# A perceiver layer on one core: the opening's loads put into one queue, and the context's channels dealt to chunks by fours

## The chip, the cores and the metric

The kernel runs on one core of a Trainium2 chip, as one launch. The metric is the device time of that core in microseconds (us). Times of the runs are given as a median. The profile is one profiled execution of the program.

## What is computed

The layer takes 256 tokens `x` of 512 channels and a context of 25088 tokens of 512 channels, all float32. It has three parts, each added to its input. The first part, cross attention, takes most of the time and is the one the change touches:

```python
def xattn(q, k, v, Wq, bq, Wk, bk, Wv, bv):      # k = v = context
    qp = q @ Wq.T + bq                            # 256 x 128
    kp = k @ Wk.T + bk                            # 25088 x 128
    vp = v @ Wv.T + bv                            # 25088 x 512
    z = sigmoid(qp @ kp.T / sqrt(128))            # 256 x 25088
    return z @ vp

x = x + xattn(layernorm(x), context, context, ...)
x = x + causal_attention(layernorm(x), ...)       # 16 heads of 64, one key and value head
x = x + mixture_of_experts(layernorm(x), ...)     # 64 experts, 8 per token, and a shared one
```

There is no softmax in the cross attention, so `z @ (v @ Wv.T)` is built as `(z @ v) @ Wv.T`: the loop over the context only sums `z @ context`, and the value weights are applied once, behind the loop.

## The kernel before, in words

**Tiles and groups.** The context is cut into 66 groups: group 0 has one block of 128 tokens, the 65 others have three blocks (J = 3) of 128 tokens. Each group needs its context twice. As `ctx_g`, tokens lie on the 128 partitions; this feeds the sum `z @ context`. As `cT_g`, channels lie on the partitions; this feeds the keys, because TensorE sums over partitions. `cT_g` has four chunks of 128 channels (ND = 4), and the keys of a group are four matmuls, one for each chunk, that are summed in PSUM: `keys(g)`, line 389.

**Two ways to `cT`.** Groups 0 and 1 are transposed by TensorE (`turn_by_pe`, line 355), which turns whole 128 x 128 blocks of `ctx_g` against the identity matrix `ident`; the result goes to PSUM, and ScalarE and VectorE copy it to `cT` (lines 377 and 379). A chunk there is 128 neighbouring channels. From group 2 on (BY_PE = 2), VectorE transposes (`turn`, line 351). For that the context is read a second time from memory, as `quarters_g` (`load_quarters`, line 123): four transfers, each of which puts a quarter of the channels (128 of them) on 32 partitions. One transpose instruction at line 353 turns all 32 x 32 squares of it: 1536 elements on each partition. There, chunk c holds channels 32c to 32c+31 of each of the four quarters.

**Two copies of the key weights.** The channels of a chunk thus differ between the two ways, and so must the rows of the key weights. `wk_plain` (line 149) has the rows in plain order and serves groups 0 and 1; `wkT_sb` (lines 154 to 159, four transfers) has them as VectorE's chunks need them, and serves the rest. `keys` picks one at line 385.

**The loop.** For each g, lines 666 to 694: VectorE's sums of context blocks (`context_sums`, the tile T) and, by GpSimd and ScalarE, the rest of them for the next group; scores `pz` (line 409) and their sigmoid on ScalarE into `zT` (line 418); the keys of the next group; the products `xacc` (line 610) of the group before, as a fast 3 x 3 scheme with fewer products that needs the sums S and T; VectorE's sums S of `zT`; the transpose for group g+2; and the loads for group g+3 at the top. `in_turn` keeps the order of the program on an engine for the instructions it wraps; what is not wrapped is placed by a scheduler.

**The opening.** `x` arrives in two halves of 128 tokens, one on the queue of SyncE (SP) and one on ScalarE's (lines 145 and 146). Then SP loads `ctx_0`, `wk_plain`, `ctx_1` (one transfer), `quarters_2`, `wkT_sb`, `ctx_2`; ScalarE's queue loads `wqT`; GpSimd's the two biases. Meanwhile TensorE multiplies zeros (`keep_warm`, line 621). VectorE finds mean and variance of both halves of `x` and normalizes them into `xn` (lines 623 to 630). TensorE turns `ctx_0` (line 631), then `xn` (line 638), whose transpose `xnT` is copied by both engines (line 643); then come the keys of group 0, the queries `pq` (line 651, four matmuls of 256 tokens) with their bias (line 660), and the transposes of `ctx_1` (line 661). The loop follows.

Of the kernel before, what the change touches and what calls it, by code (L numbers as in the profile page):

```python
# [22 lines left out]
def tile_perceiver_layer(  # L23
# [71 lines left out]

    idle_sb = cpool.tile([P, J, D], F32, tag="ctx", name="idle_sb", bufs=5)[:, 0, :]
    in_turn(nc.vector.memset(idle_sb, 0.0))

# [14 lines left out]
    def blocks_of(g):  # L115

        return range(J) if g > 0 else (1,)

    def tokens_of(g):
        lo = HEAD + (g - 1) * J * P if g > 0 else 0  # L120
        return context[lo : lo + len(blocks_of(g)) * P, :]

    def load_quarters(g):

        q = cpool.tile([P, J * P // R, D // NA], F32, tag="quarters", name=f"quarters_{g}", bufs=3)
        for a in range(NA):
            nc.sync.dma_start(
                q[a * R : (a + 1) * R, :, :],
                tokens_of(g).rearrange("(b i) (a d) -> a i b d", i=R, a=NA)[a],
            )  # L130
        quarter_tiles[g] = q

    def load_context(g):
        t = cpool.tile([P, J, D], F32, tag="ctx", name=f"ctx_{g}", bufs=5)
        blocks = blocks_of(g)
        nc.sync.dma_start(
            t[:, blocks[0] : blocks[-1] + 1, :],
            tokens_of(g).rearrange("(j p) d -> p j d", p=P),
        )
        ctx_tiles[g] = t  # L140


    BY_PE = 2
    x_sb = act.tile([P, NT, D], F32, tag="x", name="x_sb")
    for t, queue in enumerate((nc.sync, nc.scalar)):
        queue.dma_start(x_sb[:, t, :], x[t * P : (t + 1) * P, :])
    load_context(0)
    wqT_sb = load("wqT", [P, ND, QK], rows(wqT), queue=nc.scalar)
    wk_plain_sb = load("wk_plain", [P, ND, QK], rows(wkT), cpool)
    bk_sb = load("bk", [QK, 1], bk, queue=nc.gpsimd)  # L150
    bq_sb = load("bq", [QK, 1], bq, queue=nc.gpsimd)
    load_context(1)
    load_quarters(2)
    wkT_sb = const.tile([P, ND, QK], F32, tag="wkT", name="wkT_sb")
    for a in range(NA):
        nc.sync.dma_start(
            wkT_sb[a * R : (a + 1) * R, :, :],
            wkT.rearrange("(a c r) e -> a r c e", a=NA, r=R)[a],
        )
    load_context(2)  # L160


    def later(name, shape, *parts, halves=False):
# [68 lines left out]

    ident = const.tile([P, P], F32, tag="ident", name="ident")
    make_identity(nc, ident)
    eps_sb = const.tile([P, 1], F32, tag="eps", name="eps_sb")
    nc.vector.memset(eps_sb, EPS)
    ones_sb = const.tile([P, 1], BF16, tag="ones", name="ones_sb")
    nc.vector.memset(ones_sb, 1.0)

# [15 lines left out]
    token_n = const.tile([P, NT], mybir.dt.int32, tag="token_n", name="token_n")  # L255
    nc.gpsimd.iota(token_n, pattern=[[P, NT]], base=0, channel_multiplier=1)
    tokens_sb = const.tile([P, NT], BF16, tag="tokens", name="tokens_sb")
    const.tile([P, 16], F32, tag="spacer", name="spacer")
    nc.gpsimd.tensor_copy(tokens_sb, token_n)

    tri = const.tile([P, 2, P], F32, tag="tri", name="tri")
# [88 lines left out]

    def turn(g):
        q = quarter_tiles.pop(g)
        in_turn(nc.vector.transpose(new_turned(g), q.rearrange("p b (c r) -> p c b r", r=R)))  # L353

    def turn_by_pe(g):

        cT = new_turned(g)
        blocks = blocks_of(g)
        n = len(blocks)

        many = 512 // (n * P)
        for lo in range(0, ND, many):
            pt = sum_bank(f"ptc_{g}_{lo}")[:, 0 : many * n * P]
            for c in range(lo, lo + many):
                for i, k in enumerate(blocks):
                    at = ((c - lo) * n + i) * P
                    in_turn(
                        nc.tensor.transpose(
                            pt[:, at : at + P],
                            ctx_tiles[g][:, k, c * P : (c + 1) * P],  # L370
                            ident,
                        )
                    )
            to = cT[:, lo : lo + many, 0 : n * P // R, :]
            src = pt.rearrange("p (c b r) -> p c b r", c=many, r=R)
            if lo % 2:
                in_turn(nc.vector.tensor_copy(to, src))
            else:
                in_turn(nc.scalar.copy(to, src))

    def keys(g):

        cT = turned_tiles.pop(g)
        n = len(blocks_of(g)) * P
        w = wkT_sb if g >= BY_PE else wk_plain_sb
        pk = keys_bank(f"pk_{g}")[:, 0:n]
        for c in range(ND):
            in_turn(
                nc.tensor.matmul(  # L389
                    pk,  # L390
                    lhsT=w[:, c, :],
                    rhs=cT[:, c, 0 : n // R, :].rearrange("p b r -> p (b r)"),
                    start=(c == 0),
                    stop=(c == ND - 1),
                )
            )
        kT = cpool.tile([QK, J * P], F32, tag="kT", name=f"kT_{g}")

        for lo, hi in ((0, P), (P, n)) if 0 < g < 3 else ((0, n),):
            in_turn(nc.scalar.activation(kT[:, lo:hi], pk[:, lo:hi], AF.Identity, bias=bk_sb))  # L400
        return kT
# [217 lines left out]
            opened.add(i)  # L619

    keep_warm(D, D, 3 * P)
    xn = work.tile([P, NT, D], F32, tag="tok", name="xn")
    found = [moments(x_sb[:, t, :], f"x{t}") for t in range(NT)]
    for t, (mean, sd, rs) in enumerate(found):
        in_turn(nc.vector.reciprocal(rs, sd))
        in_turn(
            nc.vector.tensor_scalar(
                xn[:, t, :], x_sb[:, t, :], mean, rs, ALU.subtract, ALU.mult
            )
        )  # L630
    turn_by_pe(0)
    xnT = work.tile([P, ND, T], F32, tag="tokT", name="xnT")
    pxs = [sum_bank(f"pt_xn_{c}") for c in range(0, ND, 2)]
    for t in range(NT):
        for c in range(ND):
            at = (c % 2) * T + t * P
            in_turn(
                nc.tensor.transpose(
                    pxs[c // 2][:, at : at + P], xn[:, t, c * P : (c + 1) * P], ident
                )  # L640
            )
    for i, copy in enumerate((nc.vector.tensor_copy, nc.scalar.copy)):
        in_turn(copy(xnT[:, 2 * i : 2 * i + 2, :].rearrange("p c t -> p (c t)"), pxs[i]))

    warm = small.tile([P, 1], F32, tag="warm", name="warm_0", bufs=1)
    in_turn(nc.scalar.activation(warm, eps_sb, AF.Sigmoid))
    kT = keys(0)
    pq = sum_bank("pq")
    for c in range(ND):
        in_turn(  # L650
            nc.tensor.matmul(
                pq[:, :T],
                lhsT=wqT_sb[:, c, :],
                rhs=xnT[:, c, :],
                start=(c == 0),
                stop=(c == ND - 1),
            )
        )
    qT = cpool.tile([QK, T], F32, tag="qT", name="qT", bufs=1)
    in_turn(nc.vector.tensor_scalar(qT, pq[:, :T], bq_sb, None, ALU.add))  # L660
    turn_by_pe(1)
    open_products()


# [1611 lines left out]
```

## Time and profile before

| what | before |
|---|---|
| median of 3 runs | 750.83 us (750.47 to 751.04) |
| the profiled execution's own time | 751.11 us |
| its span (first to last instruction) | 749.2 us |
| TensorE matmul busy (PE) | 742.1 us (99%) |
| TensorE weight load busy (PEld) | 615.9 us (82%) |
| VectorE busy (DVE) | 598.2 us (80%) |
| ScalarE busy (ACT) | 209.5 us (28%) |
| GpSimd busy (POOL) | 210.1 us (28%) |
| moved by DMA | 148.66 MB, mean 198 GB/s |
| granted TensorE clock, mean | 1.000 |

How to read it: a row of groups names line, engine, operation, output and inputs, shapes and how often, then busy us and mean ns of one, then the engine's idle time just before them and what ended it. A row of the timeline is start, duration, engine, line, operation and how many were merged, with the idle time before it in brackets. A row of the windows has PE, PEld, DVE, ACT and POOL busy us (and instructions), the granted clock, the DMA engines' share and GB/s. PE overlaps PEld. The ends of matmuls are modelled, so that a busy PE need not be at its peak, and the matmuls of a row may overlap.

### The profile page before, as it was taken

How to read it: one execution, taken by the hardware profiler on the slowest of the kernel's cores; microseconds unless marked ns; L12 is line 12 of the kernel's file. 1: busy time of each engine (PE TensorE's matmuls, PEld its weight loads, DVE VectorE, ACT ScalarE, POOL GpSimd, SP SyncE). 2: the span in 40 equal slices, each digit the busy share in tenths (PEclk: the TensorE clock that was granted, in tenths of full speed). 3: DMA queues.
4: the chain of work that ended last, by engine and by line, in shares of the span. 5: the costliest groups of instructions: out<-in, count | busy, mean ns of one | idle time of the engine just before them, and what ended most of it. 6: DMA issues, size and time to landing. Idle time of an engine off the chain costs nothing.

```text
span 749.2 us, 12967 instructions
## 1 busy us (share of the span) xinstructions
PE 742.1 (99%) x4238; PEld 615.9 (82%) x4238; DVE 598.2 (80%) x1733; ACT 209.5 (28%) x509; POOL 210.1 (28%) x406
## 2 busy tenths in 40 slices
PE   8999999999999999999999999999999999999997
PEld 6888888888888888888888888888878679987775
DVE  5987888788788878888887888788776678986576
ACT  4222222222222222222222222222236632112110
POOL 3222232223223222322222222223212610561451
PEclk9999999999999999999999999999999999999999
DMA  9998877887799999999987887885034005998762
GB/s 247 269 238 212 199 185 180 210 199 172 197 257 210 219 207 250 256 224 211 227 196 199 202 189 171 212 199 136 1 108 146 2 29 193 389 384 278 271 180 82
DMA packets 156165, 148.66 MB, mean 198 GB/s; under 512 B 8326, under 2 KB 113939, under 8 KB 156096
## 3 DMA queue, kind: packets, MB, share of 16 engines
q1 hardware_dynamic: 153184, 140.28, 74.5%
q0 software_dynamic: 2240, 7.02, 2.9%
q8 instruction: 34, 0.56, 0.3%
q10 hardware_dynamic: 672, 0.52, 0.2%
q14 instruction: 35, 0.29, 0.2%
HBM read 145.63 MB, written 2.16 MB: 197 GB/s over the span
## 4 chain that ended last, share of the span: by engine, by line
PE 97%; DMA 1%; DVE 1%; SPq 0%; ACT 0%; issue 0%
PE xacc L610 38%; PE pk L389 22%; PE pz L409 11%; PE ph_e L1489 5%; PE seven L1611 4%; PE pa L1014 2%; PE ph_few L2039 2%; PE pw L1086 2%; PE ph_s L1489 2%; DMA ctx<-in_context 1%; PE po_few L2069 1%; PE ph_first L1408 1%; PE pd_last L1680 1%; PE ph_second L1408 1%; PE ph_e L1408 1%; PE ps L1112 1%
## 5 line engine op out<-in xcount | busy, mean ns | idle before, releaser
L610 PE MATMUL xacc<-T,S 128*128 128x172 f32 (+2 forms) x912 | 185.5, 308 | 0.0
L389 PE MATMUL pk<-cT,wkT_sb 128*128 128x384 f32 x512 | 175.5, 486 | 0.0
L610 PEld LDWEIGHTS xacc<-T,S 128*128 128x128 f32 x912 | 152.5, 190 | 20.1
L389 PEld LDWEIGHTS pk<-cT,wkT_sb 128*128 128x128 f32 x512 | 97.1, 190 | 54.4
L577 POOL TENSOR_TENSOR T<-ctx 128x172 f32<-128x172 f32 x65 | 31.9, 491 | 382.3 <-PE xacc L610 376.0
L577 DVE TENSOR_TENSOR T<-ctx 128x172 f32<-128x172 f32 (+1 forms) x262 | 113.8, 435 | 0.0
L353 DVE STREAM_TRANSPOSE cT<-quarters 128x1536 f32<-128x1536 f32 x64 | 113.3, 1771 | 0.3 <-issue 0.3
L577 DVE TENSOR_TENSOR S<-zT 128x128 f32<-128x128 f32 x196 | 56.4, 288 | 71.0 <-ACT zT L418 71.0
L409 PE MATMUL pz<-qT,kT 128*128 128x256 f32 x392 | 106.1, 379 | 0.0
L418 ACT ACTIVATE zT<-pz 128x256 f32<-128x256 f32 (+1 forms) x131 | 64.2, 490 | 113.6 <-PE pz L409 113.6
L610 PE MATMUL xacc<-T,zT 128*128 128x173 f32 (+1 forms) x396 | 89.9, 308 | 0.0
L400 ACT ACTIVATE kT<-pk,bk 128x384 f32<-128x384 f32 (+2 forms) x68 | 38.4, 568 | 146.9 <-PE pk L389 146.9
L610 PE MATMUL xacc<-ctx,S 128*128 128x172 f32 x392 | 78.5, 309 | 0.0
L587 ACT COPY T<-ctx 128x170 f32<-128x170 f32 (+1 forms) x130 | 43.4, 336 | 124.8 <-PE xacc L610 123.4
L577 DVE TENSOR_TENSOR S<-zT,S 128x128 f32<-128x128 f32 x325 | 76.3, 284 | 0.0
L577 POOL TENSOR_TENSOR T<-ctx,T 128x170 f32<-128x170 f32 (+1 forms) x130 | 72.4, 575 | 0.0
L577 DVE TENSOR_TENSOR T<-ctx,T 128x172 f32<-128x172 f32 x195 | 65.4, 361 | 8.2 <-PE xacc L610 1.5
L409 PEld LDWEIGHTS pz<-qT,kT 128*128 128x128 f32 x392 | 68.5, 190 | 3.8 <-ACT kT L400 0.2
L610 PEld LDWEIGHTS xacc<-T,zT 128*128 128x128 f32 x396 | 66.4, 190 | 0.3
L610 PEld LDWEIGHTS xacc<-ctx,S 128*128 128x128 f32 x392 | 62.8, 190 | 0.1
L610 PE MATMUL xacc<-ctx,zT 128*128 128x170 f32 (+1 forms) x264 | 59.5, 307 | 0.0
L610 PEld LDWEIGHTS xacc<-ctx,zT 128*128 128x128 f32 x264 | 44.3, 189 | 0.3
(355 smaller groups left out, 846.6 us busy)
## 6 DMA issues: line engine op xcount, KB each, us to landing
ctx<-in_context SPq DMA_DIRECT2D x65, 768.0 KB, 5.3
quarters<-in_context SPq DMA_DIRECT2D x256, 192.0 KB, 6.8
gu<-in_e_gate_up SPq DMA_DIRECT2D x12, 1024.0 KB, 9.3
gu_s<-in_s_gate_up SPq DMA_DIRECT2D x8, 512.0 KB, 11.4
dn<-in_e_down SPq DMA_DIRECT2D x7, 512.0 KB
a_wqT<-in_a_wqT SPq DMA_DIRECT2D x4, 512.0 KB
a_wout<-in_a_woutT SPq DMA_DIRECT2D x2, 1024.0 KB
dn_s<-in_s_down SPq DMA_DIRECT2D x4, 512.0 KB
```

Source lines behind the costliest of these rows:

```text
L353: in_turn(nc.vector.transpose(new_turned(g), q.rearrange("p b (c r) -> p c b r", r=R)))
L389: nc.tensor.matmul(pk, lhsT=w[:, c, :], rhs=cT[:, c, 0 : n // R, :].rearrange("p b r -> p (b r)"), start=(c == 0), stop=(c == ND - 1),)
L400: in_turn(nc.scalar.activation(kT[:, lo:hi], pk[:, lo:hi], AF.Identity, bias=bk_sb))
L409: nc.tensor.matmul(pz[:, i * T : (i + 1) * T], lhsT=kT[:, at : at + P], rhs=qT, start=True, stop=True,)
L418: nc.scalar.activation(zT[:, blocks[0] : blocks[-1] + 1, :].rearrange("p j t -> p (j t)"), pz[:, 0 : len(blocks) * T], AF.Sigmoid, scale=1 ...
L577: in_turn(f(o_, a_, b_))
L587: in_turn(nc.scalar.copy(named[to][:, 0:n], named[x_][:, 0:n]))
L610: nc.tensor.matmul(banks_of_products[i][:, cols], lhsT=named[lhs], rhs=named[rhs][:, 0:n],  start=i not in opened, stop=(g == G - 1 and last),
L1014: nc.tensor.matmul(pa[:, 0 : hi - lo], lhsT=a_wqT_sb[:, c, e * P : (e + 1) * P], rhs=anT[:, c, lo:hi], start=(c == 0), stop=(c == ND - 1),)
L1408: nc.tensor.matmul(ph[:, f * T + lo : f * T + hi], lhsT=gu[:, c, col : col + P], rhs=fT[:, c, lo:hi], start=(c == 0), stop=(c == ND - 1),)
L1489: nc.tensor.matmul(to[:, f * P : (f + 1) * P], lhsT=lhs[:, c, f * P : (f + 1) * P], rhs=rhs[:, c, :], start=(c == 0), stop=(c == HALVES - 1),)
L1611: nc.tensor.matmul(product_of_seven(nm), lhsT=block(n, hT, dn, s_, t_, lhs), rhs=block(n, hT, dn, s_, t_, rhs),  start=(n == SEVEN[0] and ...
```

## The change

Three things are changed.

The loads of the opening go into one queue, SP's, and keep the order of the program: both halves of `x`, `ctx_0`, the key weights, the query weights, the three blocks of `ctx_1` as three transfers, `quarters_2`, `ctx_2`. The loads up to group 5 keep their order too. The query and key weights are read with four neighbouring rows to a partition.

A chunk of channels is now every fourth channel: chunk c holds channels c, c+4, c+8 and so on. TensorE's transposes of the opening read `ctx` and `xn` with a step of four floats; VectorE's transpose reads each quarter with a step of four floats in place of runs of 32. Its output is as before. Since all groups have the same chunks, one copy of the key weights is left.

The opening's work is cut anew: `xn`, `xnT` and the queries go by halves of 128 tokens; `ctx_1` is turned block by block, with copies shared out by block; a dummy square root is run on ScalarE at the start, and the dummy sigmoid comes after the keys' copy of group 0. A spacer in the constants is halved.

```diff
-    for t, queue in enumerate((nc.sync, nc.scalar)):
-        queue.dma_start(x_sb[:, t, :], x[t * P : (t + 1) * P, :])
+    for t in range(NT):
+        in_turn(nc.sync.dma_start(x_sb[:, t, :], x[t * P : (t + 1) * P, :]))
     load_context(0)
-    wqT_sb = load("wqT", [P, ND, QK], rows(wqT), queue=nc.scalar)
-    wk_plain_sb = load("wk_plain", [P, ND, QK], rows(wkT), cpool)
+    wkT_sb = const.tile([P, ND, QK], F32, tag="wkT", name="wkT_sb")
+    in_turn(nc.sync.dma_start(wkT_sb, wkT.rearrange("(p c) e -> p c e", c=ND)))
+    wqT_sb = const.tile([P, ND, QK], F32, tag="wqT", name="wqT_sb")
+    in_turn(nc.sync.dma_start(wqT_sb, wqT.rearrange("(p c) e -> p c e", c=ND)))
+    ctx_tiles[1] = cpool.tile([P, J, D], F32, tag="ctx", name="ctx_1", bufs=5)
+    for k in blocks_of(1):
+        in_turn(nc.sync.dma_start(ctx_tiles[1][:, k, :], tokens_of(1)[k * P : (k + 1) * P, :]))
+    load_quarters(2)
+    load_context(2)
     bk_sb = load("bk", [QK, 1], bk, queue=nc.gpsimd)
     bq_sb = load("bq", [QK, 1], bq, queue=nc.gpsimd)
-    load_context(1)
-    load_quarters(2)
-    wkT_sb = const.tile([P, ND, QK], F32, tag="wkT", name="wkT_sb")
-    for a in range(NA):
-        nc.sync.dma_start(
-            wkT_sb[a * R : (a + 1) * R, :, :],
-            wkT.rearrange("(a c r) e -> a r c e", a=NA, r=R)[a],
-        )
-    load_context(2)
+    warm_sd = small.tile([P, 1], F32, tag="warm_sd", name="warm_sd", bufs=1)
+    in_turn(nc.scalar.activation(warm_sd, eps_sb, AF.Sqrt))
...
-    const.tile([P, 16], F32, tag="spacer", name="spacer")
+    const.tile([P, 8], F32, tag="spacer", name="spacer")
...
     def turn(g):
         q = quarter_tiles.pop(g)
-        in_turn(nc.vector.transpose(new_turned(g), q.rearrange("p b (c r) -> p c b r", r=R)))
+        in_turn(nc.vector.transpose(new_turned(g), q.rearrange("p b (r c) -> p c b r", r=R)))
...
+    def turn_by_pe(g, copies):
...
+        for i, k in enumerate(blocks):
+            pt = sum_bank(f"ptc_{g}_{k}")
+            parts = ctx_tiles[g][:, k, :].rearrange("p (d c) -> p c d", c=ND)
+            for c in range(ND):
+                in_turn(nc.tensor.transpose(pt[:, c * P : (c + 1) * P], parts[:, c], ident))
+            src = pt.rearrange("p (c b r) -> p c b r", c=ND, r=R)
+            for lo, hi, copy in copies[i]:
+                to = cT[:, lo:hi, i * P // R : (i + 1) * P // R, :]
+                in_turn(copy(to, src[:, lo:hi]))
...
-        w = wkT_sb if g >= BY_PE else wk_plain_sb
...
-                    lhsT=w[:, c, :],
+                    lhsT=wkT_sb[:, c, :],
...
+    def turn_xn(t):
+        pt = sum_bank(f"pt_xn_{t}")
+        parts = xn[:, t, :].rearrange("p (d c) -> p c d", c=ND)
+        for c in range(ND):
+            in_turn(nc.tensor.transpose(pt[:, c * P : (c + 1) * P], parts[:, c], ident))
+        pc = pt.rearrange("p (c q) -> p c q", c=ND)
+        for lo, hi, copy in (
+            ((0, ND, by_act),) if t == 0 else ((0, ND // 2, by_vector), (ND // 2, ND, by_act))
+        ):
+            in_turn(copy(xnT[:, lo:hi, t * P : (t + 1) * P], pc[:, lo:hi]))
...
+    turn_by_pe(0, [((0, ND, by_act),)])
...
+    turn_xn(0)
+    turn_xn(1)
+    kT = keys(0)
     warm = small.tile([P, 1], F32, tag="warm", name="warm_0", bufs=1)
     in_turn(nc.scalar.activation(warm, eps_sb, AF.Sigmoid))
...
+    for t in range(NT):
+        tokens_ = slice(t * P, (t + 1) * P)
+        pq = sum_bank(f"pq_{t}")[:, 0:P]
+        for c in range(ND):
+            in_turn(
+                nc.tensor.matmul(
+                    pq,
+                    lhsT=wqT_sb[:, c, :],
+                    rhs=xnT[:, c, tokens_],
+                    start=(c == 0),
+                    stop=(c == ND - 1),
+                )
+            )
+        in_turn(nc.vector.tensor_scalar(qT[:, tokens_], pq, bq_sb, None, ALU.add))
+    half = ND // 2
+    turn_by_pe(
+        1,
+        [
+            ((0, ND, by_act),),
+            ((0, ND, by_vector),),
+            ((0, half, by_act), (half, ND, by_vector)),
+        ],
+    )
```

## The prediction, made before the result was known

> **What bounds the kernel now.** I read the profile in this order: page and chain for the bound, one group of the loop for the slack of each engine, the opening's timeline for what the change touches, and the DMA rate there. The page's shares of the chain, and the longest DMA piece of the chain in order of time:
>
> ```profile
> PE 97%; DMA 1%; DVE 1%; SPq 0%; ACT 0%; issue 0%
> ...
> 2.15 9.09 DMA ctx<-in_context
> ```
>
> TensorE carries the end; the one DMA piece is group 1's context, landing at 11.24 us. One group of the loop (PE, PEld, DVE, ACT, POOL busy, clock, DMA share, GB/s), then the DVE rows that matter in it:
>
> ```profile
> 100.00:108.23 8.23, 8.23 (x46) 7.01 (x45) 6.85 (x21) 2.23 (x5) 2.06 (x4) 1.00 0.81 188
> ...
> L353 DVE STREAM_TRANSPOSE cT<-quarters 128x1536 f32<-128x1536 f32 x64 | 113.3, 1771 | 0.3 <-issue 0.3
> ...
> L577 DVE TENSOR_TENSOR S<-zT 128x128 f32<-128x128 f32 x196 | 56.4, 288 | 71.0 <-ACT zT L418 71.0
> ```
>
> PE has no gap in the 8.23 us of a group, at full clock. So only two things can move the time: when this dense stream begins, and whether another engine's group grows past 8.23. VectorE is the nearest, at 6.85: it transposes once a group (1.77) and then idles for zT, 71.0 us over some 64 groups, about 1.1 each. The opening, PE and then DVE:
>
> ```profile
> 5.80 0.60 PE L368 MATMUL ptc<-ident,ctx 128*128 128x128 f32 x4
> 7.21 1.31 PE L638 MATMUL pt_xn<-ident,xn 128*128 128x128 f32 x8 [0.82 <-DVE xn L627]
> 8.36 1.06 PE L389 MATMUL pk<-cT,wk_plain 128*128 128x128 f32 x8
> 9.25 1.89 PE L651 MATMUL pq<-xnT,wqT 128*128 128x256 f32 x8
> 11.28 1.53 PE L368 MATMUL ptc<-ident,ctx 128*128 128x128 f32 x12
> 12.65 0.60 PE L409 MATMUL pz<-qT,kT 128*128 128x256 f32 x2
> 13.08 1.13 PE L389 MATMUL pk<-cT,wk_plain 128*128 128x384 f32 x3
> ...
> 4.82 0.69 DVE L281 BATCH_NORM_STATS2 st_x<-x_sb 128x6 f32<-128x512 f32 x1 [2.99 <-DMA x_sb<-in_x]
> ...
> 6.61 0.55 DVE L627 TENSOR_SCALAR xn<-x_sb,mv_x,rs_x 128x512 f32<-128x512 f32 x1
> ```
>
> PE loses 0.8 us waiting for xn, which waits for x (4.82), and about 0.25 us at 11.28 waiting for ctx_1. From 13.08 on it is dense. Whatever the opening gains is therefore the advance of that 13.08. Rates (last figure GB/s), two queues at 2 to 4 us, one queue at 8 and 15:
>
> ```profile
> 2.00:3.00 1.00, 1.00 (x2) 0.34 (x1) 0.00 (x0) 0.97 (x1) 0.99 (x5) 1.00 0.76 266
> 3.00:4.00 1.00, 1.00 (x2) 0.34 (x1) 0.00 (x0) 0.00 (x0) 1.00 (x7) 1.00 0.86 289
> 8.00:9.00 1.00, 1.00 (x10) 1.00 (x11) 0.66 (x1) 0.44 (x1) 0.00 (x0) 1.00 1.05 377
> 15.00:16.00 1.00, 1.00 (x6) 0.72 (x5) 1.00 (x1) 0.14 (x1) 0.00 (x0) 1.00 1.03 396
> ```
>
> One queue alone is not slower than two.
>
> **The change, part by part.** *One queue in order of need.* Up to ctx_1 both kernels move 2.1 MB (x 2, context 1, weights 2, ctx_1 3 pieces of 256 KB). Before, the halves of x share the engines: 0.52 MB at about 280 GB/s from 2.05 us is 1.9, data until 3.95, BN at 4.82, so 0.87 from data to use. In line, x0's 0.26 MB takes 0.95 us: data at 3.0, use at 3.9 (estimate). SP issues every 0.46 us, faster than a piece at 280 to 377 GB/s (0.94 to 0.70): the eighth goes out at 4.0 and holds nothing up. Eight pieces end at 7.6 to 9.5, landed by 8.5 to 10.4. ACT's two issues (0.41 and 0.45) disappear ahead of a table load at 1.69 that nobody waited for: nothing gained. In the built program's order each quarter transfer of group 2 now waits on SP for the transfer eight before it (x0 first, at 3.9); behind it in SP's queue stand only later loads, and over a megabyte is still queued for the DMA engines then: no cost. Group 2's quarters then land near 13, used by VectorE at about 13.5 and by PE at pk of group 2, 17.7; a slip under 2.4 us is covered.
>
> *PE's opening again.* The warm-up still ends at 5.80. Four context transposes at 0.114 each ((12.65-11.28)/12): 6.26. The first xn transpose came 2.39 after BN (7.21-4.82): 3.9+2.39 = 6.3, so PE has its data as it comes free. The second half came 0.65 later, pk 0.50 after that: 7.44. pk to pq 0.89 (9.25-8.36): 8.33. pq in two halves of four 128-column matmuls costs pk's 0.89 each, as eight of 0.222 did before (1.78): 10.11. Twelve transposes, 1.37: 11.48, ctx_1 having landed. pz starts there, 0.43 earlier than pk could: 11.91, but pk(1) now needs all three blocks copied: last transpose 11.48, ACT copy 0.2 later, 256 columns at 0.39 (from 384 at 0.48 and 512 at 0.57), so pk at 12.15. Against 13.08: **0.93 us earlier**. DVE's copies (0.69 and 0.4) end at about 12.5; pk's third pair needs the last at 13.4: hidden. The copy that waits for ACT (halves of one tile) is counted in that. The Sqrt warming and table order are hidden: kT is needed at 11.5, made before the 1.28 load near 9. If ACT loaded first, kT would come at about 10.5, still in time.
>
> *One key copy.* Four transfers of 64 KB (SP 7.15 to 11.56) vanish, 0.26 MB; pk(2) at 18.64 did not wait for them: no time, but ctx_2 gets room.
>
> *Turn with every fourth channel.* Same 1536 elements, same single instruction, 64 times; only the source's inner step goes from 1 to 4 floats, 16 bytes. No row in this trace reads so. Nearest row: the same transpose at 1.771, of which about 0.15 is fixed (T 172 elements 0.336, S 128 elements 0.288), so 1.05 ns an element. [...] I take the nearest row, 1.77: it is the same instruction, element count and destination, and its old source already jumped every 32 elements without a price that shows. [...]
>
> *24 strided PE transposes in the opening.* The data is the weight load, 0.140 in the trace with unit step; 16-byte step: between +0 and +0.14 each, at most 3.4 us, all on PE's path. I take 0, since loads of 190 ns elsewhere lie beside their matmuls; nothing in the trace settles it. Address shifts (32 or 2048 bytes), the moved eps and the spacer: 0; the loop's order on all engines is unchanged in the built program, tail included.
>
> Sum: profiled execution 751.11 (span 749.2 and 1.9 around it) - 0.93 = 750.18; the median of the runs is 0.28 lower, 750.83, so **749.9**.
>
> **The rivals.** *VectorE becomes the bound (slower).* Mechanism: the strided read makes the transpose at line 353 longer. Up to the idle 1.1 (so a transpose of about 2.9 us, 1.64 times now) zT's wait shrinks and nothing happens; +50% (2.58) is still hidden. [...] Chance 0.22.
>
> *The opening gains nothing:* x lands no earlier when alone, or the late copies of ctx_1 eat it. With BN at 4.82, pk(1) comes at 12.15+0.92 = 13.07: 750.8. Speaks for it: the first packets come at a fixed time, and 0.87 us of the wait is not data. 0.12 (750.3 to 751.2).
>
> *Strided weight loads show:* 24 times 0.07 to 0.14 is 1.7 to 3.4, so 751.6 to 753.3. 0.08, half of it within 0.2% of before.
>
> *More than the sum:* gaps of 0.2 at groups 1 and 2 close too: under 749.3. 0.05.
>
> **How the numbers follow.** Likeliest: 749.9, own range 749.3 to 750.6, chance 0.53, of which 0.07 is under 749.33. 0.2% is 1.5 us, about what a measurement can tell from no change. Faster: 0.07+0.05 = 0.12. Within: 0.46+0.12+0.04 = 0.62. Slower: 0.22+0.04 = 0.26. The range: 749.2 leaves 0.05 below; spread evenly over 765 to 781, the VectorE case has 0.15 above 770. So 749.2 to 770.
>
> **What would show it.** Right: BN of x0 near 3.9, no PE idle before xn, ctx_1's transposes at about 10.1, pk(1) at about 12.15, a group still 8.23 us, the transpose row still 1771 ns. Wrong: that row over 2900 ns with DVE's wait for zT gone and a group of 8.5 or more (VectorE); weight loads over 140 ns in the opening (strided loads); BN still near 4.8 (no gain).

## The result and the profile after

The changed kernel takes 754.46 us (median of 6 runs, 754.18 to 755.53), the kernel before 750.61 beside it (6 runs, 750.06 to 751.04). The ratio is 1.005, with a 95% interval of 1.004 to 1.006: slower by 3.85 us, where 0.9 less was forecast. The profiled execution took 754.42, its span 752.6. A second profile and set of runs of the same kernel (e12 below) gave 754.38.

The chain of the page, then one group of the loop, then the two VectorE rows that answer to those of before:

```profile
PE 94%; DVE 3%; DMA 2%; SPq 1%; issue 0%; ACT 0%; DVEq 0%
```

```profile
100.00:108.23 8.23, 8.23 (x45) 6.94 (x44) 7.99 (x21) 2.23 (x5) 2.19 (x4) 1.00 0.73 191
```

```profile
L361 DVE STREAM_TRANSPOSE cT<-quarters 128x1536 f32<-128x1536 f32 x64 | 191.5, 2993 | 0.8 <-DMA quarters<-in_context 0.8
...
L572 DVE TENSOR_TENSOR S<-zT 128x128 f32<-128x128 f32 x196 | 65.8, 336 | 21.2 <-ACT zT L413 21.1
```

Three things are to be seen. The transpose takes 2993 ns in place of 1771. VectorE's busy time in a group is 7.99 of 8.23, and its wait for `zT` has shrunk from 71.0 us to 21.1. And yet PE is still without a gap, at 8.23 us a group: in this stretch the loop took the longer transpose for nothing, so the loss must lie elsewhere. The timeline of PE after has it, in the opening and at the keys of group 3:

```profile
7.71 0.72 PE L371 MATMUL ptc<-ident,ctx 128*128 128x128 f32 x4 [1.42 <-DMA ctx<-in_context]
...
9.24 1.06 PE L384 MATMUL pk<-cT,wkT_sb 128*128 128x128 f32 x8
...
13.99 2.85 PE L384 MATMUL pk<-cT,wkT_sb 128*128 128x384 f32 x8
...
27.40 2.85 PE L384 MATMUL pk<-cT,wkT_sb 128*128 128x384 f32 x8 [1.77 <-DVE cT L361]
```

The starts of the keys, written pk(0) for those of group 0 and so on, are the milestones of everything that follows:

| start of pk, us | 0 | 1 | 2 | 3 | 4 | 5 | later |
|---|---|---|---|---|---|---|---|
| before | 8.36 | 13.08 | 18.64 | 24.46 | 32.69 | 40.92 | 8.23 a group |
| after | 9.24 | 13.99 | 19.65 | 27.40 | 36.05 | 44.39 | 8.23 a group |
| difference | 0.88 | 0.91 | 1.01 | 2.94 | 3.36 | 3.47 | 3.46 to 3.48 up to group 65 |

So the whole loss is there by 45 us: 0.91 in the opening, which was to gain that much, 2.03 up to group 3 and 0.53 in groups 4 and 5. VectorE's timeline explains the 2.03. Its first two transposes before:

```profile
14.40 1.78 DVE L353 STREAM_TRANSPOSE cT<-quarters 128x1536 f32<-128x1536 f32 x1 [0.30 <-issue]
...
21.85 1.77 DVE L353 STREAM_TRANSPOSE cT<-quarters 128x1536 f32<-128x1536 f32 x1
```

The first use of `x` and the same two transposes after:

```profile
3.55 0.69 DVE L289 BATCH_NORM_STATS2 st_x<-x_sb 128x6 f32<-128x512 f32 x1 [1.72 <-DMA x_sb<-in_x]
...
15.88 2.98 DVE L361 STREAM_TRANSPOSE cT<-quarters 128x1536 f32<-128x1536 f32 x1 [0.79 <-DMA quarters<-in_context]
...
24.44 2.90 DVE L361 STREAM_TRANSPOSE cT<-quarters 128x1536 f32<-128x1536 f32 x1
```

Before, the second ended at 23.62, 0.84 ahead of pk(3). After, the first begins 1.48 later (0.91 from the opening, and a wait of 0.79 for its quarters where before 0.30 was idle), both are longer by 1.20 and 1.13, and the second ends at 27.34: 3.72 later, less the 0.84 of slack, is 2.88; pk(3) came 2.94 later. VectorE has no idle time between these two transposes: the wait for `zT`, which was to hide the length, is not there yet. The third transpose ends at 35.99 and still makes pk(4) wait 0.15; behind group 5 no key waits.

And where the opening went: the DMA rate (last figure, GB/s) in the fifth microsecond before, then in the fifth and sixth after.

```profile
4.00:5.00 1.00, 1.00 (x2) 0.34 (x1) 0.18 (x1) 0.00 (x0) 1.00 (x5) 1.00 1.05 359
```

```profile
4.00:5.00 1.00, 1.00 (x2) 0.33 (x1) 0.96 (x3) 0.29 (x1) 1.00 (x4) 1.00 0.68 119
5.00:6.00 1.00, 1.00 (x3) 0.33 (x1) 0.89 (x6) 0.29 (x1) 0.08 (x1) 1.00 0.85 236
```

`x` came earlier than forecast (3.55), but `ctx_0` behind it came at about 7.6, not by 5.8, since the one queue fell to 119 GB/s; the two of before moved 359 in that microsecond. Between about 3.3 and 7.0 us the packets of GpSimd's queue are under way, which load the two biases, four bytes to each of 128 partitions.

### The profile page after: what moved, and what is told of

Same layout as the page of the kernel before. It is cut to its first block, busy times and chain, and to the rows that moved or that the text cites. A ratio compares the mean times of both kernels' runs of the same rounds, so it can differ in the third digit from the quotient of the medians.

```text
span 752.6 us, 12988 instructions
## 1 busy us (share of the span) xinstructions
PE 743.3 (99%) x4246; PEld 615.9 (82%) x4246; DVE 649.7 (86%) x1734; ACT 209.8 (28%) x511; POOL 206.5 (27%) x406
## 4 chain that ended last, share of the span: by engine, by line
PE 94%; DVE 3%; DMA 2%; SPq 1%; issue 0%; ACT 0%; DVEq 0%
PE xacc L605 37%; PE pk L384 21%; PE pz L404 11%; PE ph_e L1497 5%; PE seven L1619 4%; PE ph_few L2047 2%; PE pa L1022 2%; PE pw L1094 2%; PE ph_s L1497 2%; DMA quarters<-in_context 1%; PE ph_first L1416 1%; PE po_few L2077 1%; PE pd_last L1688 1%; PE ph_second L1416 1%; PE ph_e L1416 1%; DMA ctx<-in_context 1%
## 5 line engine op out<-in xcount | busy, mean ns | idle before, releaser
L361 DVE STREAM_TRANSPOSE cT<-quarters 128x1536 f32<-128x1536 f32 x64 | 191.5, 2993 | 0.8 <-DMA quarters<-in_context 0.8
L384 PE MATMUL pk<-cT,wkT_sb 128*128 128x384 f32 (+1 forms) x528 | 179.7, 483 | 1.9 <-DVE cT L361 1.9
L572 POOL TENSOR_TENSOR T<-ctx 128x172 f32<-128x172 f32 x65 | 34.8, 535 | 387.1 <-PE xacc L605 375.3
L572 DVE TENSOR_TENSOR T<-ctx 128x172 f32<-128x172 f32 (+1 forms) x262 | 86.0, 328 | 0.2
L572 DVE TENSOR_TENSOR S<-zT 128x128 f32<-128x128 f32 x196 | 65.8, 336 | 21.2 <-ACT zT L413 21.1
L572 DVE TENSOR_TENSOR T<-ctx,T 128x172 f32<-128x172 f32 x195 | 60.1, 335 | 8.2 <-PE xacc L605 1.5
L572 POOL TENSOR_TENSOR T<-ctx,T 128x170 f32<-128x170 f32 (+1 forms) x130 | 61.8, 496 | 0.0
```

The costliest lines, as they stand in the source:

```text
L384: nc.tensor.matmul(pk, lhsT=wkT_sb[:, c, :], rhs=cT[:, c, 0 : n // R, :].rearrange("p b r -> p (b r)"), start=(c == 0), stop=(c == ND - 1),)
L572: in_turn(f(o_, a_, b_))
```

## The experiments

Theory A: in the loop the long transpose is free; the loss is made once, by the first transposes, which stand without idle time ahead of pk(3), and by the late opening. Its rivals: VectorE binds the loop all along; or the opening alone is to blame. For the transpose's length, theory F, a guess that e4 puts to the test: what counts is whether two reads in a row fall on the same 16 bytes. For the opening, the bias rows (theory D) stand against the single queue as such (rival E). Theories I and J come up with e3. In the table, the times stand beside runs of the kernel before on the same chip, and the last column is the difference to before of the last group's keys in the profile. e4 and e7 do other work and have no row; nor has e14, whose one profiled execution took 761.59 us.

| run | us | ratio to before, 95% interval | pk(1) | pk(3) | end |
|---|---|---|---|---|---|
| e1 opening alone | 750.87 | 1.0 [0.9992, 1.0009] | 13.53 | 25.01 | +0.56 |
| e2 transpose alone | 753.48 | 1.0033 [1.0021, 1.0046] | 12.57 | 25.50 | +2.55 |
| e3 after, no bias loads | 754.50 | 1.005 [1.0037, 1.0063] | 12.82 | 25.47 | +3.65 |
| e5 e1, no bias loads | 750.52 | 0.9994 [0.9986, 1.0003] | 12.79 | 24.27 | -0.18 |
| e6 e1, biases by SP | 750.42 | 0.9994 [0.9985, 1.0002] | 12.93 | 25.27 | +0.92 |
| e8 before, no bias loads | 750.22 | 0.9991 [0.9982, 0.9999] | 12.36 | 23.73 | -0.72 |
| e9 before, biases by ScalarE | 751.83 | 1.0015 [1.0006, 1.0023] | 13.83 | 25.63 | +1.29 |
| e10 two first short | 751.26 | 1.0007 [0.9998, 1.0016] | 13.80 | 25.28 | +0.83 |
| e11 two first long | 752.84 | 1.0024 [1.0012, 1.0035] | 13.18 | 25.72 | +1.37 |
| e12 after again | 754.38 | 1.0038 [1.0025, 1.0051] | 13.68 | 27.19 | +4.54 |
| e13 all but the last long | 753.39 | 1.0029 [1.0016, 1.0042] | 13.90 | 26.55 | +2.64 |
| e15 biases as rows, later | 751.88 | 1.001 [0.9995, 1.0025] | 13.10 | 24.48 | +0.02 |

A single profile's opening varies. The changed kernel, e1, e10, e11, e12 and e13 have the same opening up to pk(1), and pk(1) comes between 13.18 and 13.99. So differences of some tenths in a column carry little, and the 0.91 that the opening lost is at the upper end. What follows the last keys varies too, from 213.5 to 214.8 us. Steadier is the time from pk(1) to pk(3), which leaves the opening out: 11.38 before, 11.48 in e1, e5 and e10, whose first two transposes are short; 12.93 in e2, 12.54 in e11 and 12.65 in e13, where they are long; 13.41 and 13.51 in the two profiles of the changed kernel. The first two transposes and something beside them cost time, and e13 deals with the rest.

**e1, the opening alone.** The changed kernel with the old transpose, and a second copy of the key weights laid for it:

```diff
+    wk_late_sb = cpool.tile([P, ND, QK], F32, tag="wk_late", name="wk_late_sb", bufs=1)
+    for a in range(NA):
+        in_turn(
+            nc.sync.dma_start(
+                wk_late_sb[a * R : (a + 1) * R, :, :],
+                wkT.rearrange("(a c r) e -> a r c e", a=NA, r=R)[a],
+            )
+        )
...
-        in_turn(nc.vector.transpose(new_turned(g), q.rearrange("p b (r c) -> p c b r", r=R)))
+        in_turn(nc.vector.transpose(new_turned(g), q.rearrange("p b (c r) -> p c b r", r=R)))
+        w = wk_late_sb if g >= BY_PE else wkT_sb
```

> The changed kernel, but VectorE reads runs of 32 floats as before, with a second copy of the key weights (four transfers behind the quarters of group 2) for groups 2 and later. Theory A (the loss is the late context of group 0, then two longer transposes in front of the keys of group 3): the transpose is back at 1.77 us, the keys of group 3 start about 25.5 us (before 24.46, changed 27.40), only the opening's 0.9 us stays lost: about 751.6 us. Rival B (the transposes' price is spread over the loop or sits elsewhere, the opening alone costs nothing lasting): under 751.0, or at 754 if the transposes have no part in it.

Measured: 750.87, no change from the kernel before, where A said 751.6. The number is the one of rival B, under 751.0. In the profile the keys keep a delay of 0.55 from group 2 to the end, which is within the scatter of openings, and pk(3) waits for nothing. So without the long transposes the loss is gone, and the rival that blames the opening alone falls; that the opening by itself costs a lasting 0.9 is not shown.

**e2, the transpose alone.** Before, with every fourth channel to a chunk in VectorE's transpose and in the weights:

```diff
-            wkT.rearrange("(a c r) e -> a r c e", a=NA, r=R)[a],
+            wkT.rearrange("(a r c) e -> a r c e", a=NA, r=R)[a],
-        in_turn(nc.vector.transpose(new_turned(g), q.rearrange("p b (c r) -> p c b r", r=R)))
+        in_turn(nc.vector.transpose(new_turned(g), q.rearrange("p b (r c) -> p c b r", r=R)))
```

> The kernel before, but VectorE reads every fourth channel and the key weights of groups 2 and later are laid out to match (still four transfers, the plain copy still serves groups 0 and 1). Theory A: the transpose takes 2.99 us, the first two of them end 2.4 us later than before, 0.8 of which is slack in front of the keys of group 3; with what groups 4 and 5 add, 1.6 to 2.1 us: 752.2 to 752.7 us, and a group is still 8.23 us from then on. Rival B (VectorE binds the loop): 765 us or more. Rival C (the late start of the changed kernel is needed to expose the transposes): 750.6 to 751.2.

Measured: 753.48, 0.8 above A's range and far from those of B and C, with transposes of 2982 ns. pk(1) begins 0.51 before that of before, pk(3) 1.04 after, +1.15 up to group 34; then, at groups 35 and 40, it slips twice more to +2.55. The loop is thus not as free here as in the changed kernel. VectorE's rows between 150 and 280 us show the difference: it no longer waits for `zT` at all, and the S sums take 478 ns where before they took 286.

```profile
L577 DVE TENSOR_TENSOR S<-zT 128x128 f32<-128x128 f32 x48 | 22.9, 478 | 0.0
```

**e3, the changed kernel without the bias loads.** The biases are set to zero on chip, so the bias values are left out of keys and queries:

```diff
-    bk_sb = load("bk", [QK, 1], bk, queue=nc.gpsimd)
-    bq_sb = load("bq", [QK, 1], bq, queue=nc.gpsimd)
+    nc.gpsimd.memset(bk_sb, 0.0)
+    nc.gpsimd.memset(bq_sb, 0.0)
```

> The changed kernel with the two bias loads on GpSimd's queue left out and the bias tiles set to zero instead. Theory D (these loads of 4-byte rows, under way from 3.8 to 7.2 us, hold up the context of group 0 and the weights behind it): the context's transposes start at 5.8 to 6.3 us in place of 7.7, the keys of group 1 at about 12.3 in place of 13.99; with the transposes still slow the end comes 1.2 to 1.9 us earlier: 752.6 to 753.3. Rival E (the one queue or its order is the cause): the transposes still start at about 7.7 us, time 754.4.

Measured: the rate between 4 and 6 us is 295 and 363 in place of 119 and 236, `ctx_0` is in time, and pk(1) comes 1.2 us before that of the changed kernel.

```profile
4.00:5.00 1.00, 1.00 (x2) 0.34 (x1) 0.93 (x4) 0.29 (x1) 0.00 (x0) 1.00 0.91 295
5.00:6.00 1.00, 1.00 (x3) 0.34 (x1) 0.93 (x5) 0.29 (x1) 0.00 (x0) 1.00 0.98 363
```

But the time is the same, 754.50, where D said 752.6 to 753.3. From group 5 on it stands at +1.54, and from group 35 on it slips in three steps to +3.65. VectorE's timeline around the first step:

```profile
319.61 2.97 DVE L363 STREAM_TRANSPOSE cT<-quarters 128x1536 f32<-128x1536 f32 x1
...
327.23 0.57 DVE L574 TENSOR_TENSOR S<-zT 128x128 f32<-128x128 f32 x1
327.73 0.57 DVE L574 TENSOR_TENSOR S<-zT,S 128x128 f32<-128x128 f32 x1
328.22 0.57 DVE L574 TENSOR_TENSOR S<-zT 128x128 f32<-128x128 f32 x1
328.72 2.95 DVE L363 STREAM_TRANSPOSE cT<-quarters 128x1536 f32<-128x1536 f32 x1
```

From one transpose to the next VectorE needs 9.11 us here, not 8.23, and PE then waits 0.55 for `cT`. The sums ahead of the second take 0.57 each, the double of their usual 0.28. In the profile the opening gained 1.9 us, and gave them back 300 us later. The next theory, I: a kernel that starts earlier leaves VectorE and GpSimd in another phase, where VectorE's S sums fall together with GpSimd's T sums and both take longer; then VectorE's cycle is full, and whatever disturbs it in groups 33 to 42, where the next part's weights are fetched (in the kernel before, `a_wkv` leaves SP at 281.8 us and the two transfers of `a_wout` at 303.9 and 328.6), reaches PE. Its rival, J: the long transposes and the weight fetches do it, whatever the sums do.

**e4, the step of the transpose.** The source is read with a step of 1, 2, 3 or 8 floats by turns of the group. Chunks and weights no longer agree, so the layer's values change, and with them the choice of experts; the total (776.56) can't be compared, only the rows.

```diff
-        in_turn(nc.vector.transpose(new_turned(g), q.rearrange("p b (r c) -> p c b r", r=R)))
+                nc.vector.transpose(
+                    to.rearrange("p (s n) -> p s n", s=s), flat.rearrange("p (n s) -> p s n", s=s)
+                )
```

> The changed kernel with VectorE's transposes reading the quarters' 1536 floats with a step of 1, 2, 3 or 8 floats by turns of groups, so the channels of the chunks are mixed and the output is not the layer's. Theory F (what counts is whether two reads in a row fall on the same 16 bytes): steps 1 and 2 take 1.77 us, step 8 about 2.99, step 3 between. Rival G (any step above 1 costs): step 2 is over 2.3 us. Rival H (the price grows with the step): step 8 is well over 2.99.

Measured, for steps 8, 3, 1 and 2 in this order:

```profile
L382 DVE STREAM_TRANSPOSE cT<-quarters 128x1536 f32<-128x1536 f32 x16 | 47.7, 2979 | 0.0
L375 DVE STREAM_TRANSPOSE cT<-quarters 128x1536 f32<-128x1536 f32 x16 | 36.8, 2301 | 1.3 <-DMA quarters<-in_context 1.3
L364 DVE STREAM_TRANSPOSE cT<-quarters 128x1536 f32<-128x1536 f32 x16 | 28.3, 1769 | 0.0
L368 DVE STREAM_TRANSPOSE cT<-quarters 128x1536 f32<-128x1536 f32 x16 | 28.3, 1768 | 0.0
```

Two floats are free, three cost 0.53 us, four (2993, in the changed kernel) and eight the same 1.21 to 1.22. Rivals G and H fall. The five figures fit F: with a step of 8 bytes two reads share each 16 bytes (1768 ns), with 12 only some do (2301), with 16 none (2993), and at 32 it is no worse (2979). They show the price of these steps; how VectorE fetches its source was not shown.

**e5 and e6, the opening of e1 without the bias loads, and with them on SP's queue.** e5 has e3's edit on e1 (bias values left out); e6 loads both behind `wqT_sb`:

```diff
+    in_turn(nc.sync.dma_start(bk_sb, bk))
+    in_turn(nc.sync.dma_start(bq_sb, bq))
     ctx_tiles[1] = cpool.tile([P, J, D], F32, tag="ctx", name="ctx_1", bufs=5)
```

> The opening of the changed kernel with VectorE's old transpose (runs of 32, a second copy of the key weights), and the two bias loads left out, the bias tiles being set to zero. Theory D (GpSimd's loads of 4-byte rows hold up the one queue): the keys of group 1 start at about 12.3 to 12.9 us in place of 13.53 with the loads and 13.08 before; the transposes have slack, so all of it reaches the end: 750.0 to 750.4 us against 750.87. Rival E (what the one queue gains is lost elsewhere): no earlier than 750.9.

> As the last kernel, but with both biases really loaded, on SP's queue behind the query weights. Theory D: software and hardware queue differ and these small loads cost the one queue little: within 0.3 us of the kernel without bias loads. Rival: the 4-byte rows themselves are what holds the engines, wherever they are issued: context blocks of group 1 and the keys late by about 1 us, 751 us or more.

Measured: 750.52 and 750.42 beside 750.89; neither is clear of before, and e5 is 0.1 above its forecast. In e5 pk(1) comes at 12.79. In e6 `ctx_0` is in time (TensorE's first transpose at 5.78, 336 GB/s from 4 to 5 us), but now the third block of `ctx_1` is late, 0.71 of waiting at 11.75, so pk(1) comes at 12.93. The small rows are not free in either queue; they only hold up what lies behind or beside them.

**e7, relief for VectorE.** e3 without three of the ten S sums. The 3 x 3 scheme then no longer gives the right products and the experts' part runs longer (total 960.67), so only the loop's rows count.

```diff
-        s6 s4 - a10
-        s8 a01 + s5
-        s9 a01 + a02
-        ("p13 s6 b02", "p11 s8 t6"),
+        ("p13 s5 b02", "p11 s5 t6"),
```

> The changed kernel without bias loads (e3), and with three of VectorE's ten sums of a group left out (s6, s8 and s9; the products that read them read s5 or s7), so the output is not the layer's; VectorE gets 0.6 us a group, TensorE's work is the same. Theory I (in e3 VectorE's group fills the whole 8.23 us once its sums fall together with GpSimd's, and each late load from group 35 on then moves TensorE): VectorE idles again for zT, the slips at groups 35, 40 and 45 (2.1 us together) are gone, and the keys of group 3 come earlier: 751.0 to 752.4 us. Rival J (those slips are TensorE waiting for loads, VectorE aside): they stay, 754 us.

Measured: pk(3) at 24.81, +0.46 from group 5 to group 65, and no slip at groups 35, 40 or 45, although the transposes are as long (2978) and the fetches the same. VectorE waits for `zT` again, and the sums have their short time:

```profile
L571 DVE TENSOR_TENSOR S<-zT 128x128 f32<-128x128 f32 x31 | 9.0, 289 | 14.8 <-ACT zT L415 14.8
```

J falls. Of I, that the slips need a full VectorE is shown; why the sums fall together in some kernels, and which engine holds up which, is not.

**e8 and e9, the biases of the kernel before: without them, and on ScalarE's queue.** e8 has e3's edit on before (bias values left out). e9:

```diff
-    bk_sb = load("bk", [QK, 1], bk, queue=nc.gpsimd)
-    bq_sb = load("bq", [QK, 1], bq, queue=nc.gpsimd)
+    bk_sb = load("bk", [QK, 1], bk, queue=nc.scalar)
+    bq_sb = load("bq", [QK, 1], bq, queue=nc.scalar)
```

> The kernel before, with the two bias loads left out and the bias tiles set to zero. Theory D for two queues as well: x and the context of group 1 land a little earlier, 750.2 to 750.7 us. If the loads hurt the one queue only: 750.8 to 751.1, as the kernel before.

> The kernel before with its two bias loads issued on ScalarE's queue behind the query weights, not by GpSimd; all else as before. If the four-byte rows loaded by GpSimd hold up the other loads of the opening, the time falls to about that of the kernel before without them, 750.2 to 750.5, with the keys of group 1 near 12.5 us. Rival: ScalarE's two further issues, about 0.42 us each, push its square-root table and the normalized x back by up to 0.8, or rows of four bytes slow the queue as much from there: 750.9 to 751.5.

Measured: 750.22 and 751.83. Without the rows the kernel before gains 0.7 (750.89 beside it; 0.72 at the last keys); from ScalarE's queue they cost 1.3 more (750.57 beside it). The rival held, and by more than it asked. The rate falls to 124 GB/s at 6 to 7 us, and `ctx_1` is late:

```profile
12.03 1.53 PE L368 MATMUL ptc<-ident,ctx 128*128 128x128 f32 x12 [1.10 <-DMA ctx<-in_context]
```

**e10 and e11, two transposes of 64.** Both start from e1. In e10 groups 2 and 3 alone have the short transpose and the other 62 the long one; e11 is the reverse.

```diff
+        runs = "p b (c r) -> p c b r" if g in (2, 3) else "p b (r c) -> p c b r"
+        w = wk_late_sb if g in (2, 3) else wkT_sb
```

> The changed kernel with unit-step transposes (and key weights laid to match) for groups 2 and 3 alone; the other 62 transposes keep the step of four floats. Theory that the two transposes ahead of the keys of group 3 carry the lasting loss: keys of group 3 at most 0.7 us later than before, then constant; total 751.0 to 751.5. Rival that the loss is spread over the loop, since VectorE has less idle time in each group: the delay grows behind group 3, at the latest around groups 34 to 45, and the total is 752.5 to 754.

> The reverse: the step of four floats for groups 2 and 3 alone, the other 62 transposes with unit step as before. Theory that the two first transposes carry the loss: keys of group 3 about 2.9 us and of group 5 about 3.4 later than before, then constant to the end, total 754.0 to 754.8, although 62 of 64 transposes are as short as before. Rival that the loop carries it: total 751.0 to 752.

Measured: e10 takes 751.26, as expected, and its pk(3) doesn't wait. In it 62 long transposes cost nothing that this measures, where the changed kernel with 64 is 3.85 slower: theory A stands for the changed kernel, and a loop bound by VectorE all along falls. It is not free under all conditions, as the late slips of e2 and e3 show. e11 takes 752.84, with the place as expected and the size not: the delay grows at pk(3) alone, from 0.19 to 1.26, and stays at 1.37. The expected 754.0 to 754.8 were missed by over a microsecond.

```profile
25.72 2.85 PE L394 MATMUL pk<-cT,wkT_sb 128*128 128x384 f32 x8 [0.90 <-DVE cT L370]
```

In e11 the first transpose began at 14.19 with no wait for quarters; in the changed kernel at 15.88, with 0.79. e1, e10 and e11 have four transfers between the quarters of group 2 and `ctx_2`, as the kernel before has; the changed kernel has none.

**e12 and e13, that difference.** e12 is the changed kernel once more. e13 is the changed kernel with these four transfers put back, used for group 65 alone:

```diff
+        runs = "p b (c r) -> p c b r" if g == 65 else "p b (r c) -> p c b r"
+        w = wk_late_sb if g == 65 else wkT_sb
```

> The changed kernel once more, unaltered, for a second profile of its opening. If the path of its first profile is the usual one: a context of group 0 that lands past 7.5 us, a first transpose by VectorE that waits about 0.8 us for the quarters and begins near 15.9, keys of group 3 near 27.4, total about 754.4. Rival, that the first profile was an unlucky one: first transpose near 14.2 to 14.9 without a wait, keys of group 3 near 25.7 to 26.4.

> The changed kernel with four added transfers of 64 KB (a second copy of the key weights, used for group 65 alone, which is turned with unit step) between the quarters of group 2 and the context of group 2; the other 63 transposes keep the step of four floats. Theory that the context of group 2, 768 KB right behind the quarters in the queue, holds the quarters up and so moves the first transpose back: without a wait here, keys of group 3 about 1.3 us after those of before, total 753.0 to 753.5. Rival that the added transfers do nothing: as the changed kernel, 754.2 to 754.8.

Measured: e12 takes the path of the first profile, with `ctx_0` at 7.41, the first transpose at 15.50 after 0.72 of waiting for quarters, and pk(3) at 27.19. e13 takes 753.39, its first transpose begins at 15.00 without a wait, and pk(3) comes at 26.55. With almost the same pk(1) as the changed kernel (13.90 and 13.99), its end is 0.84 earlier. So 256 KB *more* to load make the kernel faster by about 1 us. (The two intervals in the table overlap, so that the size is loose.) pk(3) itself came 2.09 after that of before, not 1.3, since the opening was late by 0.82. SP's issues of the quarters and of `ctx_2`, in the changed kernel and then in e13:

```profile
4.51 4.06 SPq L134 DMA_DIRECT2D quarters<-in_context  x4
8.89 0.40 SPq L145 DMA_DIRECT2D ctx<-in_context  x1
```

```profile
12.86 0.40 SPq L145 DMA_DIRECT2D ctx<-in_context  x1
```

The last quarter leaves SP at nearly the same time in both (8.3 and 8.2) but lands at 15.8 in one and at 14.9 in the other. What differs is what SP issues next: `ctx_2`, 768 KB, at 8.89 or four microseconds later. That it, or the quarters of group 3 issued behind it, takes the bandwidth fits; the packets were not told apart. The issue counts as well: in e3, without bias rows, SP waits less for `ctx_0`, the last quarter leaves at 6.9 and lands at 13.8, and VectorE doesn't wait, although `ctx_2` follows at once. In e6, with the four transfers, but the bias rows in SP's queue, it waits 1.04. So the four transfers are not the only condition.

```profile
15.00 2.98 DVE L370 STREAM_TRANSPOSE cT<-quarters 128x1536 f32<-128x1536 f32 x1
...
26.55 2.85 PE L394 MATMUL pk<-cT,wkT_sb 128*128 128x384 f32 x8 [1.01 <-DVE cT L370]
```

**e14 and e15, biases as rows.** The kernel before, with each bias loaded by GpSimd as one row of 512 bytes and spread over partitions by a matmul of one column; in e14 these stand behind the transposes of `ctx_0`, in e15 behind those of `xn`.

```diff
+        nc.gpsimd.dma_start(bias_row[:, i, :], b_.rearrange("q o -> o q"))
+                pb[:, i : i + 1], lhsT=bias_row[:, i, :], rhs=ident[0:1, 0:1], start=True, stop=True
+    in_turn(nc.vector.tensor_copy(bias_sb, pb))
```

> The kernel before with each bias loaded by GpSimd as one row of 512 bytes on one partition, and put on 128 partitions by two tiny matmuls behind the four transposes of group 0 and one copy by VectorE; all else as before. If the 256 four-byte rows are what delays the opening's loads, about as the kernel before without biases, with 0.1 to 0.2 us more on TensorE: 750.2 to 750.5. Rival that any load by GpSimd does it, or that the two matmuls stand in the path for more: 750.6 to 751.2.

> As the kernel before with each bias loaded as one row of 512 bytes, but the two tiny matmuls stand behind the transposes of the normalized x, where TensorE waits for copies anyway, and not behind those of the context of group 0, where they waited 0.36 and 0.45 us for their rows. If the small rows are what delays the opening's loads: keys of group 1 near 12.5 us, 750.2 to 750.5, a version a little faster than the kernel before and clear of the changed one. Rival that nothing is to be had this way: 750.6 to 751.0.

Measured: e14 751.00 beside 750.86, ratio 1.0004 [0.9992, 1.0016]; e15 751.88 beside 751.16, 1.001 [0.9995, 1.0025]. No gain: the rival held, and e15's time is even 0.9 above its range. But the rate of e15 from 5 to 7 us is 332 and 318 GB/s, where that of before is 243 and 257. So the small rows do slow the other loads, and taking them away helps those; the two matmuls (0.60 on PE's path ahead of pk) give it back. No version that loads its biases beats the kernel before beyond doubt: e8's 0.7 us needs biases that nobody loads.

## Why the prediction was wrong

Two terms were put at nothing that were not, the longer transpose and the later quarters, and a gain in the opening did not come.

*"I take the nearest row, 1.77."* This is the first step that failed. The transpose took 2.99 us, 1.69 times as long. The row was near in all but the property that was changed: its source jumped at every 32 elements, never between two neighbours. The distance of neighbouring reads is what the time went by: 1769 ns at 4 bytes and 1768 at 8, but 2301 at 12, 2993 at 16 and 2979 at 32 (e4 and the changed kernel).

*"Up to the idle 1.1 [...] zT's wait shrinks and nothing happens."* This is the second step that failed, and it is where the loss is made. It was right where it was read, at 100 us, and wrong for the first groups. At 2.99 the transpose is just at that bound, and PE's group stayed 8.23. It helped that the T sums grew shorter. In the stretch from 150 to 280 us, before and then after:

```profile
L577 DVE TENSOR_TENSOR T<-ctx 128x172 f32<-128x172 f32 x64 | 28.1, 439 | 0.0
```

```profile
L572 DVE TENSOR_TENSOR T<-ctx 128x172 f32<-128x172 f32 x64 | 20.7, 324 | 0.0
```

Four of them in a group give 0.46 back of the transpose's 1.22, and the wait for `zT` pays the rest: 17.1 to 4.9 us over 16 groups, 0.76 each. But the slack of one group of the loop was taken for that of all groups. In the first two, VectorE does the sums and transposes of the start back to back, with 0.84 of slack ahead of pk(3), and 2.33 of added length went through it. As PE is dense from there on, nothing gives it back. The range puts the rival "VectorE becomes the bound" at 765 to 781. No run shows that term: 64 transposes of 2993 ns left the group at 8.23 us, and what came in its place is an onset, paid once: the delay grows by 1.93 at pk(3), and by 0.53 more up to group 5.

*"A slip under 2.4 us is covered"* (quarters of group 2). The landing was late enough to make VectorE wait 0.79 at 15.88. It was checked against pk(2), which did not suffer; the next one late was pk(3), by way of the second transpose. The waits of SP, put at "no cost", had their part: SP stood 1.2 us for `ctx_0` before the third quarter, and the last quarter landed at 15.8, not near 13. And *"One key copy [...] no time, but ctx_2 gets room"* had the sign wrong: issuing the four transfers had put `ctx_2` off, to 12.13 on SP, where the changed kernel issues it at 8.89, with the last quarter landing at 15.8. e13 puts about 1 us on that.

*"One queue alone is not slower than two"* and the opening's 0.93. The terms on `x` (3.9, measured 3.55) and on the shape of PE's work were good; from 7.71 to 13.99 PE needed 6.28 where 6.35 was forecast (5.80 to 12.15). What failed is that the context would be there when the warm-up ended at 5.80: the queue fell to 119 GB/s, and the transposes began at 7.71. Rates at 8 and 15 us, from which the step was read, had no bias rows beside them. With the rows taken away pk(1) comes at 12.82 in e3 and at 12.34 in e7, which has the same opening: 0.26 and 0.74 better than before, still less than was forecast. (The terms given for the last step, 11.48, 0.2 and 0.39, make 12.07, not 12.15.)

*Strided weight loads at 0.* They took 0.21 in place of 0.14, in the middle of the bounds, which were an estimate from that 0.14, but the matmuls were spaced at 0.120 in place of 0.114: some 0.15 us for all 24. Taking 0 was nearly right.

*The range* of 749.2 to 770 held the time by luck: none of the rivals had the reason, and none of their sums comes to 3.85 us slower. The nearest, strided weight loads with 1.7 to 3.4, measured 0.15.

## What to carry to other kernels

Slack is a property of a place, not of an engine: before calling a longer instruction hidden, look for its first instances, where the slack of the loop may not exist yet (here an idle 1.1 us a group in the loop, and none between VectorE's first two transposes). PE, dense as it is here, did not give back what it lost once: 3.47 us at group 5, 3.46 to 3.48 up to group 65. With VectorE filled to 97%, as in e3 (3.9 us idle between 150 and 280 us), PE's delay grew from 1.54 to 3.65 us in three steps; with three sums fewer a group, in e7, none of the steps came. A row prices an edit only if it shares the property that the edit changes, here the distance of neighbouring reads (1771 and 2993 ns); and loads that look superfluous can be worth their time: with 256 KB more, the last quarter of e13 landed at 14.9, not 15.8.

## What the runs showed that was not expected

The step of VectorE's transpose is free at 8 bytes and costs 0.53 us at 12 and 1.2 at 16 and 32, for 1536 elements. VectorE's sums of 0.28 take 0.57 at some phases against GpSimd's, so that the same work fills VectorE or leaves 0.76 us idle in a group. In the changed kernel three of the last four S sums ahead of the third transpose took 0.57 to 0.58 (31.33 to 33.10 us), while GpSimd summed T (31.19 to 33.45); the same four ahead of the second took 0.28 to 0.29 (23.63 to 24.53), while GpSimd was idle. It looks like the two hindering each other, but no run measured it by itself.

One loss was followed by another. In e12 PE waited 1.87 us ahead of pk(3), and the granted clock (the figure before the DMA share) then fell to half for some 3 us:

```profile
27.00:28.00 1.00, 0.81 (x2) 0.62 (x3) 0.96 (x5) 0.00 (x0) 0.00 (x0) 0.77 1.05 212
28.00:29.00 1.00, 1.00 (x3) 0.39 (x3) 0.90 (x4) 0.00 (x0) 0.00 (x0) 0.50 1.16 346
29.00:30.00 1.00, 1.00 (x3) 0.64 (x2) 0.88 (x4) 0.00 (x0) 0.00 (x0) 0.50 1.09 196
30.00:31.00 1.00, 1.00 (x3) 0.46 (x2) 0.96 (x6) 0.00 (x0) 0.00 (x0) 0.52 1.21 207
```

The keys took 4.54 us in place of 2.85. In the first profile, after a wait of 1.77, the clock stayed at 1.00 there. It was the slowest of e12's five runs, 755.12. Two profiles don't make a threshold, and no run tested whether the wait was the cause.

What stays open: how four-byte rows slow the other loads, whether a single queue suffers more from them than two do, and which disturbance in groups 33 to 42 sets off the slips of e2 and e3.
